# A graph-network kernel on one Trainium2 core: shifted due times for the last pairs' finishing steps, and two pairs finished on VectorE

## The chip, the cores and the metric

The kernel runs on one core of one Trainium2 chip. The metric is device time in microseconds (us); lower is better. Before the change three runs took 700.36, 701.53 and 701.82 us (median 701.53). A profiled execution shows when each instruction ran on the core's engines: TensorE (PE, its weight loads PEld), VectorE (DVE), ScalarE (ACT), GpSimd (POOL) and SyncE (SP), which issues transfers.

## The reference, cut to what matters

There are 128 graphs of 128 nodes with 64 features, `x` (128, 128, 64), and a sparse `adj` (128, 128, 128). Two residual layers follow one another, each with a normalisation over the features.

```python
# layer 0
mask = adj > 0
h  = relu((x @ W1a)[:, :, None, :] + (x[:, :, None, :] - x[:, None, :, :]) @ W1b + b1)   # H = 192
hm = einsum('bjkh,bjk->bjh', h, mask)
x  = layernorm(x + hm @ W2 + deg[..., None] * b2)
# layer 1
agg = einsum('bmn,bnd->bmd', adj, x)
h = elu(agg @ W1 + b1)
h = elu(h @ W2 + b2)
x = layernorm(x + h @ W3 + b3)
```

## The kernel before

Graphs are taken in pairs: 64 pairs, numbered 0 to 63. For each pair the nodes are sorted by their number of neighbours, so that a block of nodes with few neighbours needs few slots. There are nine blocks to a pair (`BLOCKS`, L43). A pair passes through these threads of steps, each a Python generator that yields one step at a time (engine, estimated cost, what it waits for, PSUM banks it needs, and what it issues):

- `prepare` (L554), `sort_x` (L600) with `project_a` (L614), `sort_mask` (L664), `turn` (L703) and `project_c` (L719) count and sort, project `x`, and make the one-hot matrices `oh` on VectorE (L694), nine to a pair, one for each block. `project_a` also makes `corr`, on GpSimd (L661).
- nine units (L937), one for each block: ScalarE copies `aj` into one of three edge banks of PSUM (L945), TensorE adds the gathered rows with 18 products (L956), VectorE sums absolute values into `sums` (L966). A unit may begin once the unit three before it has been summed, since both use the same bank.
- `finish` (L871): `hm = sums - corr`; a projection on TensorE; a copy `ys`; `unsort`; a first `norm` (L756: `y`, `st`, `ve`, `rs`, then `x1`); the aggregation with `adj` (L907); `agg`; a first hidden product and `elu` (L813: `r`, `e`, `h`), a second hidden product and `elu`, the last product, a second `norm` giving `o`, and the store of `o` (L932).

Where `p < LATE`, `finish` runs `hm`, `ve`, `x1`, the sum `h` and `o` on GpSimd, with a second ScalarE relu `up` ahead of `h`. For `p >= LATE` it runs `hm`, `ve` and `x1` on VectorE, `h` in one VectorE instruction without `up`, and `o` half on ScalarE and half on VectorE; only `rs` stays on GpSimd. `LATE = NP - 1` (L754), so this is pair 63 alone.

`Flow` (L88) puts all steps of all pairs in one order, and so sets the instruction order on each engine, which the chip then follows: every engine works its own queue in order. Each thread has a table of due times, one for each step (`DUE`, L205), to which `ROUND * p` is added. While `under_way` is true, the step with the earliest due time among those whose predecessors have been placed is taken next. While it is false, the step that could start earliest by the estimated costs is taken, and due times only choose among near ones. `under_way` becomes true with the first unit and false for the last 14 units (L960). The late form of `finish` has one step more than the table has entries, and reads the table straight through.

`overflow` (L838) tests on VectorE and TensorE whether any node has more neighbours than its block has slots. It is started by the last pair's `finish` (L893), and a slow path of the program (`dense`) runs only if the test says so.

Of the kernel before, what the change touches and what calls it, by code (L numbers as in the profile page):

```python
# [186 lines left out]
def sparse(tc, env):  # L187

    g = type("env", (), dict(env))
    nc, P, N, F, H, O, HB, H1, NP, E = (  # L190
        g.nc, g.P, g.N, g.F, g.H, g.O, g.HB, g.H1, g.NP, g.E)
# [5 lines left out]
    flow = Flow([ps_m.tile([P, 512], F32, name=f"m{i}") for i in range(5)])  # L197
# [4 lines left out]
    ROUND = 11.1651  # L202
# [17 lines left out]
            40.82),  # L220
    }

    def begin_thread(name, p, gen):
        flow.start(ROUND * p, DUE[name], gen)

    def event(*key):
        return EV.setdefault(key, [])
# [523 lines left out]
                     lambda: nc.gpsimd.tensor_sub(flat(low), flat(rest), upper(flat(rest))))  # L751
        happened(ev, "cp", p)

    LATE = NP - 1  # L754

    def norm(p, yps, ev, name, rest, shift):  # L756


# [29 lines left out]
        def apply(v, s):  # L788
# [3 lines left out]
            else:  # L792
                v.tensor_scalar(o[:, s, :], y[:, s, :], rs[:, s:s + 1], None, op0=OP.mult)
        if p < LATE:
            ev, = yield ("POOL", 1.1, [ev] + made("mhalf"), 0,
# [17 lines left out]
    def elu(p, zb, ev, name, k):  # L813
# [10 lines left out]
        h = work.tile([P, 2 * N], F32, name=name)  # L824
        if p < LATE:
            up = work.tile([P, 2 * N], F32, name="up", bufs=3)
# [11 lines left out]
    def overflow():  # L838


        v, B = nc.vector, 2 * NP

        over = slotc[:, :NB * B].rearrange("p (n b) -> p n b", n=NB)

        def before():
            for i, (p0, p1, sl) in enumerate(BLOCKS):
                v.memset(first[:, i:i + 1], float(p0))
        ev, = yield ("DVE", 0.5, [[0.0]], 0, before)

        def compare(blocks):  # L850
            for i in blocks:
                v.tensor_scalar(over[:, i, :], g.degs, float(BLOCKS[i][2]), None, op0=OP.is_gt)
        for k in range(0, NB, 3):
            ev, = yield ("DVE PORT", 0.5, [ev], 0, lambda: compare(range(k, k + 3)))

        def rows_over(t):
            for i in range(NB):
                nc.tensor.matmul(t[:B, i:i + 1], over[:, i, :], onesb[:, 0:1], start=True, stop=True)
        ev, t = yield ("PE", 0.6, [ev], 1, rows_over)
        ev, = yield ("DVE", 0.1, [ev], 0, lambda: v.tensor_tensor(hit[:B], t[:B, :NB], first[:B],  # L860
                                                                  op=OP.is_gt))
        flow.give(t, ev)
        ev, = yield ("DVE", 0.1, [ev], 0, lambda: v.tensor_reduce(bad[:B], hit[:B], AX.X, OP.max))
        ev, t = yield ("PE", 0.1, [ev], 1, lambda t: nc.tensor.matmul(
            t[:1, :B], bad[:B], identb[:B, :B], start=True, stop=True))
        ev, = yield ("DVE", 0.2, [ev], 0, lambda: v.tensor_reduce(
            count, t[:1, :B].rearrange("o (n s) -> o n s", s=2), AX.X, OP.max))
        ev, = yield ("DVE", 0.2, [ev], 0, lambda: v.tensor_reduce(some, t[:1, :B], AX.X, OP.max))
        flow.give(t, ev)

    def finish(p):  # L871

        d, xx = S[p], XX[p]
        hm = work.tile([P, 3, N], F32, name="hm", bufs=4)
        late = p >= LATE
        ev, = yield ("DVE PORT" if late else "POOL PORT", 0.47 if late else 1.05,
                     [event("corr", p)] + [event("sums", p, i) for i in range(NB)], 0,
                     lambda: (nc.vector if late else nc.gpsimd).tensor_sub(hm, d["sums"], d["corr"]))  # L878

        def project(yb):  # L880
            cp, mtp = d["cp"], d["mtp"]
            tiled(yb[:, :2 * O], hm[:, 2, :], flat(w2t), start=True, stop=False)
            for s in range(2):
                tiled(yb[:, s * O:(s + 1) * O], hm[:, s, :], w2h, start=False, stop=False)
            for s in range(2):
                for i in range(3):
                    tiled(yb[:, s * O:(s + 1) * O], mtp[:, s, :], cp(i, s, slice(H, H + O)),
                          start=False, stop=(s == 1 and i == 2))
        ev, yb = yield ("PE:t", 0.65, [ev] + made("w2d"), 1, project)
        ys = work.tile([P, 2 * O], F32, name="ys")  # L890
        ev, = yield ("ACT", act(2 * O), [ev], 0, lambda: nc.scalar.copy(ys, yb[:, :2 * O]))
        flow.give(yb, ev)
        if p == NP - 1:  # L893
            due = DUE["finish"]
            flow.start(ROUND * p, [due[4]] * 4 + [due[8], due[12], due[12], due[14], due[15], due[15]],
                       overflow())

        def unsort(t):
            for s in range(2):
                tiled(t[:, s * O:(s + 1) * O], d["permT"][:, s, :], ys[:, s * O:(s + 1) * O],  # L900
                      start=True, stop=True)
        ev, t = yield ("PE:t", 0.22, [ev, event("permT", p)], 1, unsort)
        x1, ev = yield from norm(p, t, ev, "x1", xx, True)

        def aggregate(t):
            for s in range(2):
                nc.tensor.matmul(t[s * F:(s + 1) * F, :N], x1[:, s, :], d["turned"][:, s, :],  # L907
                                 start=True, stop=True)
        ev, t = yield ("PE:t", 0.22, [ev, event("turned", p)], 1, aggregate)
        agg = work.tile([P, N], F32, name="agg")  # L910
        ev, = yield ("ACT", act(N), [ev], 0, lambda: nc.scalar.copy(agg, t[:, :N]))
        flow.give(t, ev)

        def hidden1(zb):
            for s in range(2):
                tiled(zb[:, s * N:(s + 1) * N], v1p[:, s, :], agg, start=True, stop=True)
        ev, zb = yield ("PE:t", 0.43, [ev] + made("v1p"), 1, hidden1)
        h1, ev = yield from elu(p, zb, ev, "h1", 0)

        def hidden2(zb):  # L920
            tiled(zb[:, :2 * N], v2s, h1, start=True, stop=True)
        ev, zb = yield ("PE:t", 0.43, [ev], 1, hidden2)
        h2, ev = yield from elu(p, zb, ev, "h2", 1)

        def last(t):
            tiled(t[:, :2 * O], onesb[:, :P], c3p, start=True, stop=False)
            for s in range(2):
                tiled(t[:, s * O:(s + 1) * O], h2[:, s * N:(s + 1) * N], v3s,
                      start=False, stop=(s == 1))
        ev, t = yield ("PE:t", 0.3, [ev] + made("rowp", "v3s"), 1, last)  # L930
        o, ev = yield from norm(p, t, ev, "o", x1, False)
        nc.sync.dma_start(g.out[2 * p:2 * p + 2].rearrange("b j f -> j b f"), o)  # L932


    units = [(p, i) for p in range(NP) for i in range(NB)]

    def unit(u, ev):  # L937
        p, i = units[u]
        d = S[p]
        base, n, p0, p1, sl = LAY[i]  # L940
        w = p1 - p0
        e = edges[u % NE][:, :3 * n]
        ev, = yield ("ACT", 0.09 + 3 * n / 1200,
                     [ev, event("aj", p)] + made("banks"), 0,
                     lambda: nc.scalar.copy(  # L945
                         e.rearrange("p (c s w) -> p c s w", c=3, w=w),
                         d["aj"][:, :, p0:p1].rearrange("p c (o w) -> p c o w", o=1)
                         .to_broadcast([P, 3, sl, w])))

        def gather():  # L950
            cp, oh = d["cp"], d["oh"]
            for k in range(3):
                for c in range(3):
                    for h in range(2):
                        s, chunk = (c, h) if c < 2 else (h, 2)
                        nc.tensor.matmul(e[HALVES[h], c * n:(c + 1) * n],  # L956
                                         cp(k, s, slice(chunk * HB, (chunk + 1) * HB)),
                                         oh[:, 2 * base + s * n:2 * base + (s + 1) * n],
                                         start=False, stop=(k == 2), skip_group_check=True)
        flow.under_way = u < len(units) - 14  # L960
        ev, = yield ("PE:t", 0.03 + 0.0037 * n, [ev, event("cp", p), event("oh", p, i)], 0, gather)

        def reduce():
            if "sums" not in d:
                d["sums"] = work.tile([P, 3, N], F32, name="sums")
            nc.vector.tensor_reduce(d["sums"][:, :, p0:p1],  # L966
                                    e.rearrange("p (c s w) -> p c w s", c=3, w=w),
                                    AX.X, OP.add, apply_absolute_value=True)
        ev, = yield ("DVE", 0.07 + 3 * n / 960, [ev], 0, reduce)
        happened(ev, "sums", p, i)  # L970
        return ev
# [252 lines left out]
```

## Time and profile before

| what | value |
|---|---|
| three runs, median (lowest to highest) | 701.53 us (700.36 to 701.82) |
| the profiled execution | 701.58 us, span 699.8 us |
| granted TensorE clock, mean | 0.991 |
| TensorE (PE) busy | 677.0 us, 97% |
| VectorE (DVE) busy | 672.8 us, 96% |
| ScalarE (ACT) busy | 621.9 us, 89% |
| GpSimd (POOL) busy | 595.9 us, 85% |
| bytes moved by DMA | 20.02 MB, mean 29 GB/s |

The busy shares are means over the whole span. A pair takes about 10 us in the steady part, while the work of one pair from its first load to its store stretches over several such rounds, so that at any time several pairs are in different stages. At the end of the span no new pairs enter, and only the finishing of the last ones is left. A row of the timeline view gives start, duration, engine, line, operation, the tiles written and read, how many instructions were merged, and in brackets the idle time before it and what ended it.

### The profile page before, as it was taken

How to read it: one execution, taken by the hardware profiler on the slowest of the kernel's cores; microseconds unless marked ns; L12 is line 12 of the kernel's file. 1: busy time of each engine (PE TensorE's matmuls, PEld its weight loads, DVE VectorE, ACT ScalarE, POOL GpSimd, SP SyncE). 2: the span in 40 equal slices, each digit the busy share in tenths (PEclk: the TensorE clock that was granted, in tenths of full speed). 3: DMA queues.
4: the chain of work that ended last, by engine and by line, in shares of the span. 5: the costliest groups of instructions: out<-in, count | busy, mean ns of one | idle time of the engine just before them, and what ended most of it. 6: DMA issues, size and time to landing. Idle time of an engine off the chain costs nothing.

```text
span 699.8 us, 40850 instructions
## 1 busy us (share of the span) xinstructions
PE 677.0 (97%) x17245; PEld 611.1 (87%) x17246; DVE 672.8 (96%) x2259; ACT 621.9 (89%) x1732; POOL 595.9 (85%) x991
## 2 busy tenths in 40 slices
PE   7989999999999999999999999999999999999983
PEld 4878999999999999999999999999999999999972
DVE  6899999999999999999999999999999999999973
ACT  3678999999999999999999999999999999999963
POOL 5447998899898998898898989989898998998983
PEclk9999999999999999999999999999999999999996
DMA  3200101111110110111011011101101110100000
GB/s 93 56 3 3 35 23 30 35 25 28 34 34 19 33 34 24 29 34 34 19 35 33 23 31 34 34 18 34 33 20 33 34 31 21 35 22 8 12 10 19
DMA packets 54989, 20.02 MB, mean 29 GB/s; under 512 B 37904, under 2 KB 54800, under 8 KB 54800
## 3 DMA queue, kind: packets, MB, share of 16 engines
q1 hardware_dynamic: 54096, 17.06, 10.1%
q8 instruction: 137, 2.24, 1.3%
q14 instruction: 52, 0.43, 0.2%
q10 hardware_dynamic: 704, 0.30, 0.2%
HBM read 13.14 MB, written 4.19 MB: 25 GB/s over the span
## 4 chain that ended last, share of the span: by engine, by line
PE 90%; DVE 4%; POOL 2%; ACT 1%; issue 1%; DMA 1%; SPq 0%; POOLq 0%; DVEq 0%; ACTq 0%
PE e L956 46%; PE m L250 23%; PE m L728 4%; PE m L623 3%; PE m L709 3%; PE m L907 2%; PE m L619 2%; PE m L606 2%; DVE sums L966 2%; PE m L644 1%; DVE oh L694 1%; PE m L648 1%; PE m L710 1%; POOL rs L776 1%; PE m L650 0%
## 5 line engine op out<-in xcount | busy, mean ns | idle before, releaser
L945 ACT COPY e<-aj 128x504 f32<-128x504 f32 (+6 forms) x576 | 311.5, 551 | 39.7 <-DVE sums L966 37.1
L966 DVE TENSOR_REDUCE sums<-e 128x54 f32<-128x486 f32 (+8 forms) x576 | 337.9, 604 | 4.2 <-PE e L956 3.6
L956 PE MATMUL e<-oh,cf 128*64 128x168 bf16 (+6 forms) x3456 | 211.4, 229 | 4.0 <-ACT e L945 2.7
L956 PE MATMUL e<-oh,rest 128*64 128x168 bf16 (+6 forms) x3456 | 209.6, 227 | 0.0
L956 PE MATMUL e<-oh,low 128*64 128x168 bf16 (+6 forms) x3456 | 209.6, 227 | 0.0
L956 PEld LDWEIGHTS <-cf 128*64 128x64 bf16 x3456 | 150.5, 110 | 30.6 <-issue 29.0
L694 DVE TENSOR_TENSOR oh<-vp,slotc 128x336 bf16<-128x336 bf16 (+6 forms) x576 | 158.5, 329 | 0.3 <-ACT vp L687 0.3
L956 PEld LDWEIGHTS <-low 128*64 128x64 bf16 x3456 | 141.7, 110 | 0.3 <-POOL low L751 0.3
L956 PEld LDWEIGHTS <-rest 128*64 128x64 bf16 x3456 | 141.9, 110 | 0.0
L776 POOL TENSOR_TENSOR rs<-ve,mhalf 128x2 f32<-128x2 f32 x128 | 102.7, 802 | 11.3 <-DVE ve L773 0.7
L830 POOL TENSOR_TENSOR h<-up,e 128x256 f32<-128x256 f32 x126 | 97.3, 773 | 11.1 <-ACT up L828 11.0
L751 POOL TENSOR_TENSOR low<-rest 128x512 bf16<-128x512 f32 x64 | 66.7, 1042 | 9.9 <-DVE rest L747 9.9
L638 POOL TENSOR_TENSOR sa<-aj,srow 128x384 f32<-128x384 f32 x64 | 65.0, 1016 | 8.4 <-DVE perm L592 4.4
L878 POOL TENSOR_TENSOR hm<-sums,corr 128x384 f32<-128x384 f32 x63 | 63.4, 1007 | 5.3 <-DVE sums L966 0.4
L820 ACT ACTIVATE r<-m,cc 128x256 f32<-128x256 f32 x128 | 61.9, 484 | 5.7 <-PE m L250 5.6
L661 POOL TENSOR_TENSOR corr<-ea,sa 128x384 f32<-128x384 f32 x64 | 65.7, 1026 | 0.0
L828 ACT ACTIVATE up<-m,cc 128x256 f32<-128x256 f32 x126 | 59.0, 468 | 0.0
L823 ACT ACTIVATE e<-r 128x256 f32<-128x256 f32 x128 | 53.3, 416 | 2.0
L747 DVE TENSOR_TENSOR rest<-m,cf 128x256 f32<-128x256 f32 x128 | 52.2, 409 | 0.0
L773 POOL TENSOR_SCALAR ve<-st 128x2 f32<-128x2 f32 x126 | 33.7, 267 | 20.8 <-DVE st L766 9.4
L743 ACT COPY cf<-m 128x256 f32<-128x256 f32 x128 | 41.5, 377 | 6.6 <-PE m L250 1.1
L630 ACT ACTIVATE aj<-m,b1n 128x128 f32<-128x128 f32 x128 | 40.1, 365 | 3.7 <-PE m L623 2.6
(163 smaller groups left out, 1460.9 us busy)
## 6 DMA issues: line engine op xcount, KB each, us to landing
adj<-in_adj_dram SPq DMA_DIRECT2D x64, 128.0 KB, 2.6
xx<-in_x_dram SPq DMA_DIRECT2D x64, 64.0 KB, 2.2
out_dram<-o SPq DMA_DIRECT2D x64, 64.0 KB, 1.7
w1s<-in_L_gnn_W_dram ACTq DMA_DIRECT2D x2, 96.0 KB, 2.9
w2s<-in_L_gnn_W_dram ACTq DMA_DIRECT2D x2, 48.0 KB, 2.5
v2s<-in_L_gnn_W_dram SPq DMA_DIRECT2D x1, 64.0 KB, 2.2
v1d<-in_L_gnn_W_dram SPq DMA_DIRECT2D x2, 32.0 KB, 2.0
rows<-in_L_gnn_b_dram SPq DMA_DIRECT2D x1, 64.0 KB, 5.6
```

Of the source, the lines that this page charges most:

```text
L250: nc.tensor.matmul(out[h], lhsT[:, h], rhs, **kw)
L638: evs, = yield ("POOL PORT", 1.0, [have] + made("srow"), 0, lambda: nc.gpsimd.tensor_mul(sa, aj, srow))
L661: ev, = yield ("POOL PORT", 1.05, [ev, evs], 0, lambda: nc.gpsimd.tensor_sub(corr, ea, sa))
L694: lambda: nc.vector.tensor_tensor(oh[:, 2 * base:2 * (base + n)].rearrange("p (b s w) -> p b s w", b=2, w=w), vp[:, :, p0:p1].rearrange("p ...
L751: lambda: nc.gpsimd.tensor_sub(flat(low), flat(rest), upper(flat(rest))))
L776: nc.gpsimd.tensor_tensor(rs, ve, mhalf, op=OP.pow)
L820: lambda: nc.scalar.activation(r, z, AF.Relu, bias=c, scale=-1.0))
L830: ev, = yield ("POOL PORT", 0.64, [ev, evr], 0, lambda: nc.gpsimd.tensor_add(h, up, e))
L878: lambda: (nc.vector if late else nc.gpsimd).tensor_sub(hm, d["sums"], d["corr"]))
L945: lambda: nc.scalar.copy(e.rearrange("p (c s w) -> p c s w", c=3, w=w), d["aj"][:, :, p0:p1].rearrange("p c (o w) -> p c o w", o=1) .to_br ...
L956: nc.tensor.matmul(e[HALVES[h], c * n:(c + 1) * n], cp(k, s, slice(chunk * HB, (chunk + 1) * HB)), oh[:, 2 * base + s * n:2 * base + (s + ...
L966: nc.vector.tensor_reduce(d["sums"][:, :, p0:p1], e.rearrange("p (c s w) -> p c w s", c=3, w=w), AX.X, OP.add, apply_absolute_value=True)
```

## The change

`LATE` becomes `NP - 2`: pairs 62 and 63 finish in the late form. For these two a list `take` assigns a due time of the table to each of the 26 steps, so that the added steps share the due time of the step that they belong to. `LAST` shifts the due times of the last pairs' `finish`; its first entry is for pair 63, its second for pair 62, and so on to pair 58. Each entry has four shifts, by the table's place: places 0 to 3 (up to `unsort`), 4 to 7 (the first norm), 8 to 15 (aggregation to second hidden product), and 16 to 24 (the rest). The due times of `overflow` follow from pair 63's. And `under_way` stays true to the end, so that due times set the order of the last 14 units and of all that follows them, too.

```diff
+    LATE = NP - 2
+    LAST = ((-3.5, -9.4, -4.9, -1.3), (5.5, -4.3, 0.3, 7.6), (-0.9, -2.8, 3.8, 7.6), (0.1, -0.2, -0.4, 5.1), (0.0, -1.6, 0.0, 0.2), (0.0, 0.0, 0.2, 0.0))
+
     def begin_thread(name, p, gen):
-        flow.start(ROUND * p, DUE[name], gen)
+        due = DUE[name]
+        if name == "finish":
+            take = range(25)
+            if p >= LATE:
+                take = (0, 1, 2, 3, 4, 5, 6, 6, 7, 8, 9, 10, 11, 12, 14, 15, 16, 17, 19,
+                        20, 21, 22, 22, 23, 24, 24)
+            k = NP - 1 - p
+            later = LAST[k] if k < len(LAST) else (0.0,) * 4
+            due = [due[i] + later[0 if i < 4 else 1 if i < 8 else 2 if i < 16 else 3]
+                   for i in take]
+        flow.start(ROUND * p, due, gen)
...
-    LATE = NP - 1
-
...
         if p == NP - 1:
-            due = DUE["finish"]
-            flow.start(ROUND * p, [due[4]] * 4 + [due[8], due[12], due[12], due[14], due[15], due[15]],
-                       overflow())
+            due = [DUE["finish"][i] + LAST[0][2] + 0.5 for i in (8, 12, 14, 16)]
+            flow.start(ROUND * p, due[:1] * 4 + due[1:2] * 3 + due[2:3] + due[3:] * 2, overflow())
...
-        flow.under_way = u < len(units) - 14
+        flow.under_way = True
```

## The prediction

> **What bounds the kernel now.** I read first the busy time of each engine in stretches of ten microseconds (columns: stretch, length, busy PE, PEld, DVE, ACT, POOL, granted clock, DMA share, GB/s).
>
> ```profile
> 650.00:660.00 10.00, 10.00 (x275) 9.07 (x271) 9.97 (x32) 9.35 (x27) 9.02 (x14) 1.00 0.04 10
> 660.00:670.00 10.00, 10.00 (x277) 9.43 (x271) 8.84 (x22) 9.61 (x27) 9.34 (x15) 1.00 0.05 11
> 670.00:680.00 10.00, 7.50 (x176) 6.21 (x172) 7.13 (x26) 5.94 (x16) 8.40 (x15) 1.00 0.04 8
> 680.00:690.00 10.00, 6.26 (x66) 4.17 (x62) 5.78 (x23) 4.70 (x13) 6.43 (x13) 0.83 0.07 15
> 690.00:700.00 10.00, 1.75 (x24) 1.17 (x24) 2.24 (x8) 1.24 (x3) 2.12 (x5) 0.55 0.09 20
> ```
>
> Until 670 TensorE and VectorE are full: the order is worth nothing there, only the amount of work is. From 670 no engine is full, and the chain of the last pair sets the end. So two things count: when the last pair's subtraction hm can start (L878; 677.57 here), and how long it is from there to the last o (694.78 + 0.35 = 695.13). What follows, 4.67 to the end of the span, I leave alone. Next I read the timeline of TensorE, VectorE and GpSimd in this stretch.
>
> ```profile
> 670.64 0.41 PE L956 MATMUL e<-oh,cf 128*64 128x168 bf16 x6 [0.53 <-DVE oh L694]
> 671.89 0.39 PE L956 MATMUL e<-oh,cf 128*64 128x154 bf16 x6 [0.40 <-DVE oh L694]
> ...
> 665.63 0.69 DVE L966 TENSOR_REDUCE sums<-e 128x51 f32<-128x510 f32 x1 [0.63 <-PE e L956]
> 669.52 1.07 DVE L694 TENSOR_TENSOR oh<-vp,slotc 128x336 bf16<-128x336 bf16 x1
> 677.57 0.56 DVE L878 TENSOR_TENSOR hm<-sums,corr 128x384 f32<-128x384 f32 x1 [0.41 <-POOL corr L661]
> 683.59 1.46 DVE L790 TENSOR_SCALAR x<-y,st,rs 128x64 f32<-128x64 f32 x2 [0.45 <-POOL rs L776]
> ...
> 669.39 1.00 POOL L661 TENSOR_TENSOR corr<-ea,sa 128x384 f32<-128x384 f32 x1
> 683.59 1.41 POOL L830 TENSOR_TENSOR h<-up,e 128x256 f32<-128x256 f32 x2
> ```
>
> TensorE waits twice for a one-hot; hm waits for corr; and one-hot and x1 on VectorE last as long as the GpSimd operation beside them. Last the chain of waits:
>
> ```profile
> 681.54 0.71 POOL rs L776
> ...
> 682.83 0.74 POOL rs L776
> 683.57 0.03 issue
> 683.59 0.79 DVE x L790
> ...
> 686.52 1.59 PE m L250 x12
> ```
>
> The last pair's rs stands behind another pair's, and its first hidden product behind another's second one.
>
> **What the skill says.** The Trainium skill, "SBUF — State Buffer", section "SBUF: two separate sides": VectorE and GpSimd share one port pair, an exclusive lock that a two-port VectorE form, or one with two SBUF inputs, and a GpSimd operation hold for a whole instruction. The trace agrees: the one-hot took 1.07 us beside corr and 0.32 us on average between 600 and 660. "TensorE: Matmul & The Clock Gate", section "What's actually happening": after about 3.4 us of idle window TensorE's clock is halved. The trace shows 0.50 to 0.60 between 684 and 687, after a thin stretch, and 0.50 again from 691.
>
> **The change, part by part.** I built both programs and compared the order of steps on each engine; times below are the trace's durations added along these lists by hand, in pairs numbered to 63 and blocks as pair.block. The lists are alike to 657; from there to the gather of block 62.6 (662.43) neighbours are swapped while TensorE stays full: zero.
>
> *Engines.* Pair 62 moves to VectorE: hm, ve twice, x1, h twice, half of o: seven steps, about 0.5 + 2x0.17 + 0.5 + 2x0.48 + 0.25 = 2.5 us there; GpSimd loses hm 0.97, two ve with their gaps 0.5, x1 0.84, two h 1.4, o 0.36 = 4.1 us; ScalarE loses two up (0.36 each) and gains half of o (0.35). VectorE is 71% busy from 670 to 680 and 58% after: hidden, except where pair 63 stands behind it in the queue. No transfer is added; the two last stores stand in SP's queue in the same order, some 0.9 us apart against 0.37 us for an issue, so they do not queue.
>
> *Feeding the last pair.* With due times to the end, the one-hots of 63.0 to 63.6 come before the sums of 62.7. VectorE: sums 62.6 done at 664.33, seven one-hots 1.52 (the pitch at 654.75), 665.85, two sums 1.15, 667.0: when it had them before, with four one-hots fewer, since it waited 0.63 there. Then y of 61 must wait for its unsort, 667.5 to 667.7, sums 63.0 and 63.1 end at 668.58. The last two one-hots now meet corr of 62 on GpSimd (668.4 to 669.4), a race of 0.15 us. Won, sums 63.2 end at 669.7; lost, at 670.8. ScalarE then does copy 63.5, r, e, up of 60 and copy 63.6, 0.53 + 0.40 + 0.32 + 0.37 + 0.53 = 2.2: gather 63.6 starts at 672.0 or 673.0 (before 672.73). The two TensorE waits for one-hots are gone; a wait for this copy takes their place. Behind 63.6 come last of 59 (0.29), the second hidden product of 60 (0.45) and two gathers (0.65 + 0.61): 674.66 or 675.66, before 675.65. In VectorE's queue y2 of 59 stands ahead of sums 63.6 and holds it about 0.5 us, which the later gathers cover. The last sums end 1.45 after the last gather starts (0.9 + 0.55): 676.1 or 677.1. Corr 63, no longer behind a GpSimd hm and x1, ends at 676.07 or 677.07. So hm of 63 starts 1.5 or 0.5 earlier; I take the middle, **1.0**.
>
> *The chain after it.* Before it is 695.13 - 677.57 = 17.56 long. Detours in it: ys behind r, e, up of 61, 0.5; unsort behind an aggregation that waits for GpSimd's x1, 0.85; y1 and st1 behind compares of the overflow test, 0.45; rs behind o of 60, 0.2; x1 1.46 instead of 0.5, 0.95; first hidden product behind the second one of 62, 1.2; r and e behind those of 62, 0.6. Sum 4.75, leaving 12.8 of plain work and hops, some 0.95 of it from the slow clock. In the new list project, unsort, aggregate and first hidden of 63 stand ahead: those detours go. New ones: y1 of 63 stands behind x1 of 62, which starts at 678.55 beside h of 61 on GpSimd (started 678.5), is held by the port to 679.55, and so costs 1.2; h1 behind the overflow test's compares and reductions, now put there, 0.45; y2 behind y2, st2, ve2 of 62, 0.35. With 0.3 for what I missed, 2.3. Gain 4.75 - 2.3 = **2.45**.
>
> Sum 1.0 + 2.45 = 3.5. The profiled execution took 701.58 (span 699.8), the median of the runs shown is 701.53, the same. Forecast 701.58 - 3.5 = 698.1 us.
>
> Bounds: the feed lies between 0.5 and 1.5. The port delay of x1 is 0 to 1.2. The clock is not to be known: at full speed the chain's products take 0.78 + 0.23 + 0.25 + 0.45 + 0.45 + 0.29 = 2.45; all slow adds 2.45, of which 0.95 is in both, so from -0.95 to +1.5. The moved forms all have a row here.
>
> **Rivals.** *Locks miss* (0.17): the one-hots win their race and x1 of 62 gets the port: 1.5 + 2.45 + 1.2 = 5.15, 696.4. For it: VectorE wins such races too (GpSimd's ve at 677.62 took 0.57 beside hm, not 0.19). Against it: at 683.59 it lost.
>
> *Clock* (0.14): with the work spread thinner TensorE is slow in the whole chain, +1.5, and the feed gives 0.5: 701.58 - 0.5 - 2.45 + 1.5 = 700.1, no change that can be told. For it: pair 62 now has its work closer to pair 63's, and gaps of over 1 us stay. Against it: the granted clock was 1.0 till 684 with TensorE only 44 to 61% busy at 679 to 681.
>
> *Slower* (0.09): the one-hots. All nine now stand ahead of sums in a stretch in which GpSimd runs x1, sa and corr. One that is locked out costs 1.07 - 0.32 = 0.75, and VectorE holds the edge banks meanwhile. Five cancel the gain, seven of nine give 701.58 - 3.5 + 5.25 = 703.3. Against it: pair 62's nine, in the same order at 654.75, took their usual pitch, and seven of the nine now fall beside ve and rs, which did not hold them there.
>
> That the change does nothing is out: the lists differ on every compute engine. That pair 61 ends last, its last product now behind the overflow test, would need 2.5 us more than I find (687.4 against 690).
>
> **How the numbers follow.** Likeliest: 0.60, 698.1, its own range 697.0 to 699.5. With the locks missing 0.77 for faster than 0.2% (1.4 us, about what a measurement can tell), 0.14 within it, 0.09 slower. The range 696.3 to 700.6 takes in the ends of the feed, of the lock and most of the clock, and leaves out the slow case.
>
> **What would show it.** No wait of gathers for one-hots after 670; hm of 63 at 676 to 677, straight after the last sums; project and unsort of 63 with no other product between; y1 of 63 right behind a long x1; 15 us from hm to o. Wrong, if hm starts at 677.5 or later (feed), if a GpSimd operation stands beside several long one-hots (slower), if the chain is still 17 us, by its clock or by new waits, or if the last o is not pair 63's.

## The result, and the profile after

The changed kernel took 699.57 us (median of 13 runs, 698.62 to 701.05), the kernel before 701.56 us beside it (13 runs, 700.36 to 703.25). The ratio is 0.9972, with a 95% interval of 0.9963 to 0.9981: 2.0 us faster, where 3.5 had been forecast. The profiled execution took 699.37 us, with a span of 697.6.

Spans of single executions are a poor yardstick here. The gather of block 1.0 (the first block of pair 1) starts at 28.51 us in the profile before, at 28.14 in the one after, and anywhere from 28.14 to 30.13 in the fourteen profiles of this study; from there to the gather of block 62.6 all of them take 633.3 to 634.1 us, so most of the offset is carried along to the end. So the profiles are compared from a common mark: the start of the gather of block 62.6, up to which the lists hold the same work in nearly the same order. From there I read three numbers: the start of the last pair's hm (what comes before it is the feed), the end of the last o, and the difference, called the chain.

Busy time in stretches of ten microseconds, after (columns as before):

```profile
660.00:670.00 10.00, 9.77 (x262) 9.02 (x259) 9.22 (x23) 8.38 (x22) 8.91 (x14) 1.00 0.05 11
670.00:680.00 10.00, 7.06 (x176) 6.05 (x172) 7.40 (x17) 6.35 (x16) 6.29 (x12) 1.00 0.04 8
680.00:690.00 10.00, 7.70 (x85) 4.70 (x80) 7.75 (x39) 5.02 (x13) 4.54 (x9) 0.83 0.04 8
690.00:700.00 10.00, 0.30 (x6) 0.12 (x4) 1.43 (x7) 0.69 (x2) 1.38 (x2) 0.52 0.11 27
```

VectorE and TensorE do more between 680 and 690 than before and less after 690: the tail is denser. But from 670 to 680 TensorE is less busy than before (7.06 against 7.50), and so is ScalarE from 660 to 670 (8.38 against 9.61). The timelines show why; first TensorE, ScalarE and VectorE of the feed, then GpSimd beside them:

```profile
671.03 0.40 PE L966 MATMUL e<-oh,cf 128*64 128x154 bf16 x6 [0.84 <-ACT e L955]
672.72 0.41 PE L966 MATMUL e<-oh,cf 128*64 128x169 bf16 x6 [0.90 <-ACT e L955]
...
670.39 0.58 ACT L955 COPY e<-aj 128x462 f32<-128x462 f32 x1 [1.40 <-DVE sums L976]
...
668.05 1.73 DVE L707 TENSOR_TENSOR oh<-vp,slotc 128x308 bf16<-128x308 bf16 x2
673.98 0.29 DVE L772 TENSOR_TENSOR y<-m,x 128x128 f32<-128x128 f32 x1 [1.41 <-PE m L263]
677.16 1.07 DVE L889 TENSOR_TENSOR hm<-sums,corr 128x384 f32<-128x384 f32 x1 [0.24 <-POOL corr L674]
...
667.81 1.00 POOL L674 TENSOR_TENSOR corr<-ea,sa 128x384 f32<-128x384 f32 x1
668.76 0.81 POOL L841 TENSOR_TENSOR h<-up,e 128x256 f32<-128x256 f32 x1
676.11 1.02 POOL L674 TENSOR_TENSOR corr<-ea,sa 128x384 f32<-128x384 f32 x1
677.07 0.73 POOL L841 TENSOR_TENSOR h<-up,e 128x256 f32<-128x256 f32 x1
```

The two gathers (63.5 and 63.6) no longer wait for one-hots; they wait for ScalarE's copies. The first copy waits for the sums of 63.2, the second stands behind it and three steps of pair 60. The sums of 63.2 stand behind two one-hots that lasted 1.73 us together, beside corr and h on GpSimd. Later y of pair 59 stops VectorE for 1.41 us ahead of the sums of 63.6. And hm of the last pair takes 1.07 us instead of 0.56, beside an h of pair 60 that GpSimd began 0.09 us sooner. From the mark (661.75), hm starts at 15.41 us; before (mark 662.43) it was 15.14. The feed has lost 0.27 us.

The chain of waits behind hm:

```profile
679.04 0.71 POOL rs L787
...
679.78 0.72 DVE x L801
...
683.88 1.43 DVE slotc L863 x6
...
685.36 0.45 PE m L869 x3
...
686.54 1.49 PE m L263 x14
```

It runs through pair 62's rs and x1, and then through the overflow test (slotc, L863; the products L869). From hm to the end of the last o it takes 677.16 to 692.33, 15.17 us, against 17.56: 2.39 us shorter. From the mark to the last o 32.70 has become 30.58, a gain of 2.12. What follows the last o grew from 4.67 to 5.27 us, a loss of 0.60. The rest of the 2.2 us between the two spans, 0.68, lies ahead of the mark.

### The profile page after: what moved, and what is told of

It is laid out like the page before. It is cut to its first block, busy times and chain, and to the rows that moved or that the text cites. A ratio compares the mean times of both kernels' runs of the same rounds, so it can differ in the third digit from the quotient of the medians.

```text
span 697.6 us, 40860 instructions
## 1 busy us (share of the span) xinstructions
PE 676.6 (97%) x17245; PEld 610.3 (87%) x17246; DVE 674.2 (97%) x2267; ACT 621.2 (89%) x1731; POOL 583.4 (84%) x983
## 4 chain that ended last, share of the span: by engine, by line
PE 90%; DVE 4%; POOL 2%; ACT 2%; issue 1%; DMA 1%; SPq 0%; POOLq 0%; DVEq 0%; ACTq 0%
PE e L966 46%; PE m L263 23%; PE m L741 4%; PE m L636 3%; PE m L722 3%; PE m L917 2%; PE m L619 2%; PE m L632 2%; DVE sums L976 1%; PE m L657 1%; PE m L661 1%; PE m L723 1%; POOL rs L787 1%; ACT e L955 1%; DVE oh L707 1%
## 5 line engine op out<-in xcount | busy, mean ns | idle before, releaser
L966 PE MATMUL e<-oh,cf 128*64 128x162 bf16 (+6 forms) x3456 | 210.9, 229 | 4.3 <-ACT e L955 4.0
L966 PE MATMUL e<-oh,rest 128*64 128x162 bf16 (+6 forms) x3456 | 209.0, 227 | 0.0
L966 PE MATMUL e<-oh,low 128*64 128x162 bf16 (+6 forms) x3456 | 209.0, 227 | 0.0
L707 DVE TENSOR_TENSOR oh<-vp,slotc 128x336 bf16<-128x336 bf16 (+6 forms) x576 | 155.9, 325 | 0.3 <-ACT vp L700 0.3
L841 POOL TENSOR_TENSOR h<-up,e 128x256 f32<-128x256 f32 x124 | 95.9, 774 | 10.4 <-ACT up L839 10.3
L787 POOL TENSOR_TENSOR rs<-ve,mhalf 128x2 f32<-128x2 f32 x128 | 92.0, 719 | 13.9 <-DVE ve L784 3.5
```

What stands on the lines that cost most here:

```text
L707: lambda: nc.vector.tensor_tensor(oh[:, 2 * base:2 * (base + n)].rearrange("p (b s w) -> p b s w", b=2, w=w), vp[:, :, p0:p1].rearrange("p ...
L787: nc.gpsimd.tensor_tensor(rs, ve, mhalf, op=OP.pow)
L841: ev, = yield ("POOL PORT", 0.64, [ev, evr], 0, lambda: nc.gpsimd.tensor_add(h, up, e))
L966: nc.tensor.matmul(e[HALVES[h], c * n:(c + 1) * n], cp(k, s, slice(chunk * HB, (chunk + 1) * HB)), oh[:, 2 * base + s * n:2 * base + (s + ...
```

## The experiments

All kernels, with the kernel before and the changed one, read in the same way; ratios are against the kernel before on the same chip.

| kernel | ratio (95%) | hm from mark | chain | last o from mark | clock in the chain |
|---|---|---|---|---|---|
| before | 1 | 15.14 | 17.56 | 32.70 | 0.79 |
| changed | 0.9972 (0.9963 to 0.9981) | 15.41 | 15.17 | 30.58 | 0.81 |
| due times to the end, alone | 1.0065 (1.0051 to 1.0078) | 16.25 | 21.66 | 37.91 | 0.55 |
| due times, two pairs, no shifts | 1.0076 (1.0063 to 1.0090) | 17.71 | 19.48 | 37.19 | 0.65 |
| due times and shifts, one pair | 1.0003 (0.9994 to 1.0012) | 16.23 | 15.69 | 31.92 | 0.92 |
| two pairs, alone | 0.9954 (0.9940 to 0.9968) | 14.25 | 14.91 | 29.16 | 0.89 |
| two pairs and shifts, order by start | 0.9952 (0.9939 to 0.9966) | 14.34 | 14.19 | 28.53 | 0.92 |
| hm of pair 62 alone | 0.9961 (0.9946 to 0.9976) | 14.26 | 16.92 | 31.18 | 0.64 |
| changed, one-hots early | 0.9956 (0.9942 to 0.9970) | 14.48 | 14.73 | 29.21 | 0.87 |
| the same and last of 59 early | 0.9964 (0.9952 to 0.9975) | 14.30 | 14.57 | 28.87 | 0.87 |
| changed, test later | 0.9968 (0.9958 to 0.9979) | 15.40 | 14.07 | 29.47 | 0.97 |
| changed, x1 of 62 later | 1.0001 (0.9989 to 1.0013) | 15.62 | 15.28 | 30.90 | 0.86 |
| changed, three edits | 0.9937 (0.9923 to 0.9951) | 14.29 | 13.91 | 28.20 | 0.90 |
| two pairs, test later | 0.9946 (0.9932 to 0.9961) | 14.26 | 14.48 | 28.74 | 0.89 |

The last column is the mean granted clock of TensorE from hm to the last o. From the mark to hm it was 1.00 in all fourteen profiles, so the starts of hm can be compared as they stand. The chains cannot: where the clock was 0.50, a second hidden product took 1.07 to 1.12 us instead of 0.60 to 0.65, and each profile is a single execution. The clock differs between executions of one program, too. Of 42 runs of the kernel before on one chip, the eleven with a mean clock of 0.994 over the span took 699.52 to 701.34 us, and the ten with 0.984 to 0.987 took 701.78 to 703.22. No run holds the clock fixed. How much of a shorter chain is shorter queues, and how much is the clock, which may itself follow from the denser work, stays open. The ratios hold both.

Of the ways to combine the three parts (two pairs, shifts, due times to the end), only the shifts alone were not run.

### One part alone: the order by due times

The kernel before, with one line changed:

```diff
-        flow.under_way = u < len(units) - 14
+        flow.under_way = True
```

> The kernel before with one line changed: due times set the order to the end (one pair on VectorE, no shifts). Theory (the gain is in the chain after the last hm, where the shifted times put pair 63 ahead of others): unshifted due times put pair 63 behind 61 and 62 in every queue, so the chain from hm to the last o gets longer than 17.6 us, and the kernel slower by 1 to 4 us. Rival (the order by due time alone is the gain, since it feeds the one-hots early): 1 to 2 us faster.

It is 4.7 us slower (706.45 against 701.78), more than the 1 to 4 of the theory. The last o comes 37.91 us after the mark. VectorE and GpSimd in this kernel:

```profile
679.14 0.56 DVE L878 TENSOR_TENSOR hm<-sums,corr 128x384 f32<-128x384 f32 x1 [2.55 <-POOL corr L661]
685.81 0.29 DVE L761 TENSOR_TENSOR y<-m,xx 128x128 f32<-128x128 f32 x1 [5.19 <-ACT agg L911]
...
678.11 1.00 POOL L661 TENSOR_TENSOR corr<-ea,sa 128x384 f32<-128x384 f32 x1
```

corr of the last pair stands on GpSimd behind x1 of 61 and h of 60, so hm waits 2.55 us for it; and y of 63 comes more than 6 us after hm, since on TensorE its projection stands behind the second hidden product of 61, and its unsort behind the aggregation of 62. Due times made for a pair in the middle of the span put the last pair last. How much of this chain's length is the clock (0.55) is not set apart. The rival falls: sums ended earlier than before (13.71 from the mark against 14.19), and it was no use.

### The shifts taken out, with two pairs

On the changed kernel:

```diff
-    LAST = ((-3.5, -9.4, -4.9, -1.3), (5.5, -4.3, 0.3, 7.6), (-0.9, -2.8, 3.8, 7.6), (0.1, -0.2, -0.4, 5.1), (0.0, -1.6, 0.0, 0.2), (0.0, 0.0, 0.2, 0.0))
+    LAST = ((0.0,) * 4,)
```

> The changed kernel with all shifts zero: two pairs on VectorE, due times to the end. Theory (shifts make the gain): pair 63 behind 61 and 62 in the queues, chain over 17.6 us, slower than before by 1 to 4 us. Rival (shifts are worth little): ratio 0.997 to 0.998.

The theory had the direction, but the loss, 5.5 us (707.26 against 701.78), is above its 1 to 4. The overflow test's due times, which follow from the shifts, are the new ones without their shift. hm waits 2.55 us for corr here too:

```profile
681.35 0.56 DVE L889 TENSOR_TENSOR hm<-sums,corr 128x384 f32<-128x384 f32 x1 [2.55 <-POOL corr L674]
```

### One part taken out: pair 62 back on GpSimd

On the changed kernel:

```diff
-    LATE = NP - 2
+    LATE = NP - 1
```

> The changed kernel with pair 63 alone on VectorE (pair 62's steps stay on GpSimd), shifts and due times to the end as changed. Theory (relieving GpSimd's queue is part of the gain): rs of 63 stands behind hm, x1 and h of 62 on GpSimd, chain 1 to 2 us longer than in the changed kernel, about as long as before: ratio 0.999 to 1.001. Rival (the shifts are all of it): ratio 0.997.

The ratio is the theory's, 1.0003, no change from the kernel before, but not for its reason. It had the chain as long as before; the chain was 15.69, 0.5 us longer than in the changed kernel, at a clock of 0.92. What is lost is lost ahead of it: hm started at 16.23, behind corr, which stands behind pair 62's hm on GpSimd. Due times and shifts together, which I had priced at nearly the whole gain, are worth nothing without the second pair on VectorE. The trace alone shows 0.8 us less than before from mark to last o; the times do not.

```profile
676.59 0.99 POOL L889 TENSOR_TENSOR hm<-sums,corr 128x384 f32<-128x384 f32 x1
677.90 1.00 POOL L674 TENSOR_TENSOR corr<-ea,sa 128x384 f32<-128x384 f32 x1
...
678.93 1.07 DVE L889 TENSOR_TENSOR hm<-sums,corr 128x384 f32<-128x384 f32 x1 [1.06 <-POOL corr L674]
```

### One part alone: two pairs on VectorE

The kernel before with the second pair moved, the due times of both pairs assigned by the list `take`, no shifts, the order of the last units by estimated start as before:

```diff
-    LATE = NP - 1
+    LATE = NP - 2
...
+        if name == "finish" and p >= LATE:
+            due = [due[i] for i in (0, 1, 2, 3, 4, 5, 6, 6, 7, 8, 9, 10, 11, 12, 14, 15, 16, 17, 19,
+                                    20, 21, 22, 22, 23, 24, 24)]
```

> The kernel before with two pairs finishing on VectorE and nothing else: the order of the last 14 units still goes by estimated start. Theory (the order by shifted times makes the chain short): x1 of 63 no longer stands beside GpSimd's h of 62, some 0.5 to 1 us gained, but hm of 62 on VectorE stands ahead of the sums of 63.4: ratio 0.999 to 1.001. Rival (the move to VectorE is the gain): ratio 0.997.

The rival held, and more: 698.28 us against 701.78, ratio 0.9954. By the ratio this one part gains more than the whole change (0.9972), though the intervals overlap a little. hm starts 0.9 us earlier, and the chain is 2.65 us shorter, at a clock of 0.89 instead of 0.79:

```profile
676.02 1.00 POOL L667 TENSOR_TENSOR corr<-ea,sa 128x384 f32<-128x384 f32 x1
676.98 0.72 POOL L835 TENSOR_TENSOR h<-up,e 128x256 f32<-128x256 f32 x1
...
677.05 1.06 DVE L883 TENSOR_TENSOR hm<-sums,corr 128x384 f32<-128x384 f32 x1
683.36 0.53 DVE L795 TENSOR_SCALAR x<-y,st,rs 128x64 f32<-128x64 f32 x2
```

corr is done a little after the last sums; x1 of 63 takes 0.53 us, not 1.46, since no h of pair 62 runs on GpSimd. hm still meets the port (1.06).

### Two pairs and shifts, order by start

The changed kernel with the one line put back:

```diff
-        flow.under_way = True
+        flow.under_way = u < len(units) - 14
```

> The changed kernel with one line put back: the last 14 units go by estimated start again; two pairs on VectorE and the shifts stay. Theory (following due times to the end is what costs, the move to VectorE is what gains): close to two pairs alone, last o at 29 to 29.6 us after the gather of 62.6, ratio about 0.9955. Rival (the shifts are made for the due order and hurt the other): 31 us or more, ratio 0.998 to 1.

The theory held: ratio 0.9952, last o at 28.53, in the profiles some 2 us ahead of the changed kernel and by the ratios 1.4, the intervals overlapping a little. So with the shifts in both, following due times to the end costs 1.07 us in the feed (14.34 against 15.41). The chain is 0.98 longer (15.17 against 14.19), of which the clock (0.81 against 0.92) has a share. Without due times to the end, the times do not tell the kernel with the shifts (0.9952) from the one without (0.9954).

### A single step moved: hm of pair 62

On the kernel before, in `finish`, where `late` decides on hm alone:

```diff
-        late = p >= LATE
+        late = p >= LATE - 1
```

> The kernel before with one step moved: hm of pair 62 runs on VectorE, all its other steps stay on GpSimd. Theory (what the move gains in the feed is this 0.97 us of GpSimd ahead of corr of 63): hm of 63 starts about 14.3 us after the gather of 62.6 instead of 15.14, the chain stays near 17.5 us, ratio about 0.9988. Rival (the gain is in the chain alone): hm at 15.1, no change. Second rival (hm on VectorE delays the sums of 63.4): hm at 15.5 or later.

hm of 63 started at 14.26 from the mark (663.95), as expected; the chain was 16.92. The last o at 31.18 is 1.5 us earlier than before; the ratio, 0.9961, says 1.7 to 3.8 us, more than this trace and more than the 0.9988 expected. The clock goes with it: three of the nine runs had a mean clock of 0.996 and took 697.54 to 698.80 us, the other six 0.986 to 0.990 and 700.07 to 701.45, and the trace is of one of the six. In the feed, where the clock was 1.00, the one step that stood ahead of corr on GpSimd is all that the move gains (14.26 against 14.25):

```profile
677.18 1.00 POOL L661 TENSOR_TENSOR corr<-ea,sa 128x384 f32<-128x384 f32 x1
...
678.21 1.06 DVE L878 TENSOR_TENSOR hm<-sums,corr 128x384 f32<-128x384 f32 x1
```

### The feed: the two one-hots out of the port's way

The changed kernel with the last pair's one-hots for blocks 7 and 8 due earlier:

```diff
+        if name == "sort_mask" and p == NP - 1:
+            due = (*due[:12], -5.12, -5.12)
```

> The changed kernel, with the last pair's two last one-hots (blocks 7 and 8) due before the sums of block 62.7, so that they no longer stand beside GpSimd's sa, corr and h. Theory (the feed lost its gain to the port lock on these two one-hots): they take about 0.5 us together instead of 1.73, ScalarE no longer waits 1.4 us for the sums of 63.2, hm of the last pair starts about 1 us earlier counted from the gather of 62.6, and the ratio to the kernel before falls from 0.997 to about 0.9957. Rival (TensorE, full in the feed, sets hm anyway, and corr on GpSimd ends last): the one-hots get short but hm starts no earlier, ratio 0.997.

The theory held. Nine one-hots in a row took 2.14 us, beside ve and rs on GpSimd, and hm started 0.93 us earlier; ratio 0.9956.

```profile
665.07 2.14 DVE L709 TENSOR_TENSOR oh<-vp,slotc 128x324 bf16<-128x324 bf16 x9
```

With the shift of pair 59's last steps changed as well, so that its last product fills a gap of TensorE ahead of the gather of 63.6:

```diff
-    LAST = (..., (0.0, -1.6, 0.0, 0.2), (0.0, 0.0, 0.2, 0.0))
+    LAST = (..., (0.0, -1.6, 0.0, -0.1), (0.0, 0.0, 0.2, 0.0))
```

> As the one-hots run, and the last product of pair 59 due just before the gather of 63.6 instead of just after it, so that VectorE does not stop for y2 of 59 (1.41 us in the changed kernel) ahead of the sums of 63.6. Theory (in-order stops on VectorE set the start of hm): another 0.3 us earlier, ratio about 0.9953. Rival (the last gathers on TensorE cover that stop): as the one-hots run, within 0.1 us.

The stop of VectorE ahead of y of 59 is gone, and hm starts 0.18 us earlier, between the theory (0.3) and the rival (under 0.1). Here hm came before h on GpSimd and took its plain time:

```profile
671.96 0.28 DVE L774 TENSOR_TENSOR y<-m,x 128x128 f32<-128x128 f32 x1
676.15 0.56 DVE L891 TENSOR_TENSOR hm<-sums,corr 128x384 f32<-128x384 f32 x1 [0.32 <-POOL corr L676]
```

The times do not tell these two apart (0.9956 and 0.9964, intervals overlapping).

### The chain: the overflow test later

```diff
-            flow.start(ROUND * p, due[:1] * 4 + due[1:2] * 3 + due[2:3] + due[3:] * 2, overflow())
+            flow.start(ROUND * p, due[:1] * 4 + [due[1] + 1.6] * 3 + [due[2] + 6.0] + [due[3] + 6.0] * 2, overflow())
```

> The changed kernel, with the overflow test's second half due after the last pair's first h, and its last product after the last pair's second hidden product. Theory (the chain's remaining detours are queueing behind other work): h1 of 63 starts at once after its exponential, 0.75 us earlier, the second hidden product no longer stands behind the test and the last product of 61, and the end comes 0.8 to 1.1 us earlier, ratio about 0.996. Rival (pair 62, whose steps end just ahead of pair 63's, sets the end, or the flag of the test now comes last): at most 0.3 us, ratio 0.9968.

In the trace the chain is 1.10 us shorter, 14.07: h of 63 starts just behind the test's compares and its second hidden product behind h. First the changed kernel's product, then the two steps here:

```profile
686.94 1.07 PE L263 MATMUL m<-h,v2s 128*64 128x256 f32 x4
...
686.93 0.47 DVE L844 SCALAR_TENSOR_TENSOR h<-m,cc,e 128x256 f32<-128x256 f32 x1
...
687.48 0.62 PE L263 MATMUL m<-h,v2s 128*64 128x256 f32 x4
```

Counted from hm, that product starts 0.88 us earlier (8.90 against 9.78), which is the queueing of the theory. It also lasts 0.62 us instead of 1.07, and the last product 0.45 instead of 0.70, since the clock was still 1.00; and 0.5 us are lost again, since y of 63 now stands behind the test's last reductions and pair 62's y, st and ve. So the 1.10 us are not the queueing alone. The ratio, 0.9968, is the rival's, and its interval (0.9958 to 0.9979) holds both. The times alone do not settle it; the sum with the feed, below, does better.

### The chain: x1 of pair 62 behind y of pair 63

On the changed kernel, pair 62's second shift:

```diff
-    LAST = ((-3.5, -9.4, -4.9, -1.3), (5.5, -4.3, 0.3, 7.6), ...)
+    LAST = ((-3.5, -9.4, -4.9, -1.3), (5.5, -0.5, 0.3, 7.6), ...)
```

> The changed kernel, with x1 of pair 62 due later, behind y1, st1 and ve1 of pair 63 on VectorE. Theory (y1 of 63 standing behind a port-locked x1 of 62 costs 0.65 us here): the chain of 63 is 0.6 us shorter, ratio about 0.9963. Rival (what 63 gains, 62 loses, and 62's second hidden product stands ahead of 63's): no gain or up to 0.5 us slower, ratio 0.997 to 0.998.

The rival held, and it was worse than it said: 1.0001, no faster than the kernel before. x1 of 63 came 0.5 us earlier counted from hm (4.60 against 5.09), but h of 63 later (9.76 against 8.97):

```profile
682.98 0.53 DVE L801 TENSOR_SCALAR x<-y,st,rs 128x64 f32<-128x64 f32 x2
683.96 0.52 DVE L801 TENSOR_SCALAR x<-y,st,rs 128x64 f32<-128x64 f32 x2
686.74 0.48 DVE L844 SCALAR_TENSOR_TENSOR h<-m,cc,e 128x256 f32<-128x256 f32 x1 [2.26 <-ACT e L834]
689.12 0.47 DVE L844 SCALAR_TENSOR_TENSOR h<-m,cc,e 128x256 f32<-128x256 f32 x1
```

The first x1 and the first h are pair 62's. They stand ahead of pair 63's steps in the later queues. Counted from hm, h of 62 came 1.33 us later than in the changed kernel (7.38 against 6.05). About half of that is the moved x1, since the aggregation behind it starts 0.61 later; the other half is the clock, 0.50 from 684.4 to 686.4 where the changed kernel had 1.00 (aggregation 0.91 us instead of 0.66, first hidden product 1.12 instead of 0.66). So that holding back 62 holds back 63 is shown only in part. The trace shows only 0.3 us lost from mark to last o, the times 2 us against the changed kernel; the profiled execution had a late start (30.13 at the gather of 1.0), and the rest stays open.

### Combinations

The three edits together, as their diffs above have them (one-hots, last of 59, test later), on the changed kernel:

> The changed kernel with three of the earlier edits together: the last pair's last one-hots early, the last product of 59 ahead of the gather of 63.6, and the overflow test's second half later. Theory (feed and chain are separate terms that add up): hm of 63 starts 14.3 us after the gather of 62.6, the chain is about 14.0 us, the last o comes 28.2 to 28.5 us after that gather (32.70 before, 30.58 changed), ratio about 0.9945. Rival (the two share what they save, since pair 62 and the sums take over): no better than the one-hots run, 28.9 us, 0.9957.

The terms add up: hm at 14.29, chain 13.91, last o at 28.20. It has the lowest ratio of the study, 0.9937 (0.9923 to 0.9951; 697.84 us against 702.22), 2.5 us further than the changed kernel. Without the test's edit it was 0.9964 (0.9952 to 0.9975), so here the times show the later test as a gain, too.

And the test later on two pairs alone:

```diff
-            flow.start(ROUND * p, [due[4]] * 4 + [due[8], due[12], due[12], due[14], due[15], due[15]],
+            flow.start(ROUND * p, [due[16] + 4.0] * 4 + [due[18] + 1.0] * 3 + [due[19]] * 3,
```

> Two pairs on VectorE with the order by estimated start, as in that run, and the overflow test's steps due later, so that x1 of 63 and its aggregation come ahead of h of 62 and of the last product of 61. Theory (the queueing of pair 63's steps behind the test and behind 61 and 62 is what is left): last o at 28.3 to 28.8 us after the gather of 62.6, ratio about 0.9945. Rival (there the test lies in gaps): 29.2 us, 0.9954.

Last o at 28.74, as the theory had it; the ratio 0.9946 is not told apart from two pairs alone (0.9954), nor from the three edits together (0.9937).

## Why the prediction was right, and where it was wrong

The side and the range were right: 699.57 lies between 696.3 and 700.6, just outside the likeliest case's 697.0 to 699.5, and pair 63 ends last. The size was not: 2.0 us of 3.5. That it came out no smaller is partly luck: of the 2.2 us between the two profiles 0.68 lie ahead of the mark, where the prediction had zero.

The step that failed is the feed, "I take the middle, 1.0". It measured -0.27. By the prediction's own sign, hm at 677.5 or later, the feed was wrong: 15.41 after the mark of the profile before is 677.84. The mechanism was the one named: the last two one-hots met corr, the race was lost, and the wait for a copy took the place of the wait for one-hots. But the lost race was priced as still 0.5 us ahead of the kernel before, with hm at 677.1 - 662.43 = 14.67. Of the 0.74 us between that and 15.41, 0.40 were lost up to the gather of 63.6: it came 10.97 us after the mark where the working says 673.0 - 662.43 = 10.57, since the two one-hots, held by two GpSimd operations one after the other, took 1.73 us, so that the first copy came 0.27 later than worked out, and the copies and the steps between them took 0.13 more. The other 0.34 came behind it, where the last product of 59, its norm and corr of 63 wait for one another: from the gather of 63.6 to the end of corr it took 677.13 - 672.72 = 4.41 us, where the working has 677.07 - 673.0 = 4.07. The run with the one-hots moved gives back 0.93 us. The middle of two outcomes is no forecast where the list shows who is in front: corr was already running (667.81) when the first one-hot came (668.05), and the working has it so, too (668.4 against 668.58).

One step of the feed's sum is wrong by itself: 674.66 and 675.66 are the ends of the last gather, while the 1.45 us are counted from its start, so the last sums would end 0.61 us earlier than worked out. It cost nothing, since corr, worked out apart, ends as late (676.07 or 677.07), and hm waits for both.

The chain, "Gain 4.75 - 2.3 = 2.45", measured 2.39. That is right as a sum and only partly by its parts, so some of it is luck. y1 behind x1 of 62 cost at most 0.67 and not 1.2 (unsort's result was there at 679.50 + 0.45 = 679.95, y1 began at 680.62); h1 behind the overflow test cost 0.76 (685.37 to 686.13) and not 0.45; y2 behind pair 62's last norm cost next to nothing and not 0.35. In their place came hm itself, held 0.5 us by the port, and the second hidden product behind the test and the last product of 61, 0.34. The clock was much the same in both chains (0.79 and 0.81).

What the prediction did not see is which part of the change makes the gain. It put the chain's detours down to the new order. By the runs, the new order costs 4.7 us when it stands alone, and with its shifts and one pair on VectorE it comes out even; two pairs on VectorE alone gain 3.2 us by the ratio (0.9954 x 701.56 = 698.3). In the sum of parts the move to VectorE has no term of its own. VectorE's load is called "hidden", and what GpSimd loses, 4.1 us by the same count, comes in only in passing, in corr of 63 "no longer behind a GpSimd hm and x1" and in the long x1. It was on the path: hm of 62 stood ahead of corr of 63, and h of 62 stood beside x1 of 63.

The tail after the last o, "I leave alone", is 0.6 us longer in this pair of profiles.

The rivals: *locks miss* was wrong for this kernel, and the runs with early one-hots, with hm 0.66 and 0.84 us earlier than before, show about half of its feed of 1.5. *Clock* did not decide between these two profiles: the granted clock from 680 to 690 was 0.83 in both. *Slower*: two of the nine one-hots were held, not seven; the other seven took 1.67 us against 1.52 worked out.

## What to carry to other kernels

When work moves from one engine to another, look first at the queue that it leaves: what stood behind it there may be on the path. Here that was worth more than the load on the engine that it went to. In the drain at the end of this pipeline, an order made for the steady part put the last item last in the queues that set the end. And a chain read from one profile holds that execution's clock: compare it only with chains at a like clock, or trust the times of many runs.

## What the hardware showed that I had not expected

The port between VectorE and GpSimd is decided by less than 0.1 us and cost half a microsecond here: hm took 1.07 us when h on GpSimd began 0.09 us before it, and 0.55 to 0.56 when it did not. It also works the other way: before the change ve on GpSimd at 677.62 took 0.56 us beside hm instead of 0.19. The Trainium skill, "SBUF — State Buffer", section "SBUF: two separate sides", says that whichever of the two starts first has the shared pair for its whole instruction, VectorE operations with two SBUF inputs among them; the trace agrees, and these numbers are what it costs here.

The granted clock fell to 0.50 without a long idle stretch. Before the change TensorE was busy 28 to 100% of each microsecond from 677 to 684, and its longest wait was 1.05 us; the clock was 0.60 from 684 to 685 and 0.50 from 685 to 687. So the idle window of about 3.4 us that the prediction takes from the skill does not stand ahead of this fall, and which share of busy time decides is not shown.

The time from the last o to the end of the span was 4.57 to 4.78 us in the four profiles with pair 63 alone in the late form and 4.86 to 5.36 in the ten with two pairs. No run tells why.

The start of the program, up to the gather of block 1.0, differed by up to 2.0 us between profiles, as much as the whole gain.
